# Two attention layers on one core: values of a chunk in one beat, layer-1 products in the other

## The chip, the core and the metric

The kernel runs on one core of a Trainium2 chip. The metric is the device time in microseconds (us) of one execution. A core has five engines with a queue each: TensorE (PE in the profile, with its weight loads as PEld), VectorE (DVE), ScalarE (ACT), GpSimd (POOL) and SyncE (SP), which here issues nearly all DMAs. Every engine works through its own queue in order and waits, by semaphores, for the others. Matmul results land in PSUM, from which VectorE and ScalarE read; everything else is in SBUF.

## The reference

The input x is 8 batches x 2048 nodes x 256 features in fp32, with one 2048 x 2048 adjacency matrix for all batches. Two layers follow, each x = layernorm(x + layer(x, adj)).

```
# layer 0: 4 heads of 64; softmax inside each chunk of 256 keys, summed over the 8 chunks
scores = clip(einsum('bhnd,bhjcd->bhnjc', q, kc) / 8, -10, 10)
scores = where(mask == 0, -10, scores)
ctx    = einsum('bhnjc,bhjcd->bhnd', softmax(scores, axis=-1), vc)
out    = layernorm(ctx @ Wo.T + bo + x) * gamma + beta
# layer 1: graph attention, one softmax over all 2048 neighbours
Wh = h @ W
e  = leaky_relu(s_i[:, :, None] + s_j[:, None, :], 0.2), -inf where not adjacent
out = elu(softmax(e) @ Wh)
```

## The kernel before

**Layer 0.** Work is cut into J = batch x block of 512 queries x chunk of 256 keys: 8 x 4 x 8 = 256 pairs of beats. A beat handles half a chunk, 128 keys, for all 4 heads and 512 queries; the first half of a chunk is the even beat (`half == 0`), the second the odd one. In each beat:

- TensorE computes transposed scores `sc` (L682): keys on partitions, two heads side by side in the array (64 rows each), two PSUM tiles `sc` of 128 x 1024 (2 buffers in all, so the next beat's first tile waits for this beat's first exponential and the second for the second);
- VectorE clips and masks each tile with one instruction against the mask `mk`, the "cap" (L692);
- ScalarE takes the exponential of each into `e` (L695).

What the exponentials of a chunk are multiplied with comes one pair later (`prev`): three column-tiled products (4 heads x 32 columns, L708), each 16 matmul passes into one PSUM tile `m` of 128 x 512. Part 2 multiplies by ones and gives the denominators; parts 0 and 1 are the two 32-wide halves of the values. Before, parts 2 and 0 run in the even beat, part 1 in the odd. The pool `ps_m` of `m` has two buffers, shared by everything else that needs a PSUM tile for a moment: projections (`pq`, `pk`, `pv`, `po`, `pw`), transposes (`pt`, `psj`, `pab`), row sums (`pr`). ScalarE copies part 2 to `ds` (L722) and parts 0 and 1 to `un` (L716). The denominators then go through a DMA into a dense layout `dc` (L724), VectorE's reciprocal at the end of the even beat (L730), DMAs to HBM `rd` and back, spread over partitions, `r` (L732, L736); two beats later VectorE scales `un` by `r` (L743), and POOL adds it to the context `ctxT` (L744).

**Layer 1** runs one batch behind, in steps (class `Step`), one for 128 keys x 512 queries; 16 steps make a block, 4 blocks a batch. `begin_beat` hands out 1.5 steps a beat (1.1 in the last batch), that is one and two in turn. A step goes through four stages, in successive beats: `low` (ScalarE, L517) in the beat it is taken; `leaky` and `edges` (VectorE, L521 and L526) in the next, before and behind the caps; `weights` (ScalarE exponential, L530, and the POOL sum `acc`, L539) at the start of the third; `product` (TensorE, L549; L564 in the last batch) at the end of that third beat, in `end_beat`. The step's tile `w` comes from a pool of 5 buffers. Products of a block add up in one PSUM tile `us` (pool `ps_u`, one buffer). With a block's last product ScalarE copies `us` to `hx` (L575), and generators in the list `fins` finish the block in later beats. Generators in `ahead` (`prelude`) prepare a batch's layer 1; between a batch's last block and the next batch's first step, layer 1 is idle for some 18 to 20 of 64 beats.

**What sets the order.** There is no scheduler (`manual_schedule`): each engine's queue has the instructions in the order in which Python emits them. Within a beat that is: `begin_beat` (weights, lows, leakies), scores, caps, exponentials, `middle_of_beat` (edges), value products with their copies, `end_beat` (products, one step of each generator, then what is due in `agenda`). So ScalarE's queue in an even beat holds weights, lows, exponential, exponential, copy `ds`, copy `un`.

Of the kernel before, what the change touches and what calls it, by code (L numbers as in the profile page):

```python
# [9 lines left out]
F32 = mybir.dt.float32  # L10
# [3 lines left out]
AF = mybir.ActivationFunctionType  # L14
# [5 lines left out]
P = 128  # L20
# [8 lines left out]
def tile_adj_attention__then__gat(  # L29
# [35 lines left out]
    nc = tc.nc  # L65
    B, N, F = x.shape
    H, D = 4, 64
# [3 lines left out]
    IB = 512  # L71
    NIB = N // IB
    TPB = IB // P
    NPAIR = H // 2
# [12 lines left out]
    one = ctx.enter_context(tc.tile_pool(name="one", bufs=1))  # L87
    two = ctx.enter_context(tc.tile_pool(name="two", bufs=2))
    three = ctx.enter_context(tc.tile_pool(name="three", bufs=3))
    five = ctx.enter_context(tc.tile_pool(name="five", bufs=5))  # L90
    eight = ctx.enter_context(tc.tile_pool(name="eight", bufs=8))
    ctx.enter_context(tc.manual_schedule())

# [413 lines left out]
    class Step:  # L507
# [5 lines left out]

        def low(self):
            k, c = self.k, self.c
            self.w = five.tile([P, IB], F32, tag="w", name=f"w{self.name}")
            nc.scalar.activation(self.w, k["ab"][:, 1, :], AF.Identity, bias=k["sj"][:, 1, c : c + 1])  # L517

        def leaky(self):
# [77 lines left out]
    def at(when, fn):  # L597
        agenda.setdefault(when, []).append(fn)

    def begin_beat(rate):  # L600
        nonlocal l1_live, credit, lows, edged, weighted, leaking
        weighted, edged = edged, []
        for s in weighted:
            s.weights()
        leaking, lows = lows, []
        credit = min(credit + rate, 2.0)
        while l1_live and credit >= 1.0:
            s = next(l1, False)
            if s is False:
                l1_live = False  # L610
            elif s is None:
                break
            else:
                credit -= 1.0
                lows.append(s)
                s.low()
        for s in leaking:
            s.leaky()
# [4 lines left out]
            s.edges()  # L623
        edged = leaking

    def end_beat():

        nonlocal weighted
        for s in weighted:
            s.product()  # L630
        weighted = []
        for gens in (ahead, fins):
            for g in list(gens):
                if next(g, g) is g:
                    gens.remove(g)
        for fn in agenda.pop(beat, []):
            fn()

    leaking = []


    first_m0 = two.tile([P, HT, IB], I8, tag="mask0", name="mk0_0_0_0")
# [7 lines left out]
    fins.append(far_made())  # L650

    prev = None
    v = None
    total = B * NIB * NCH
    mk0 = {}
    for J in range(total + 1):
# [5 lines left out]
        for half in range(2):  # L662
            c = 2 * j + half
            if live:

                if c % HT == 0:
                    if b == 0:
                        mk = blocks0[ib, c // HT]
                    else:
                        mk = mk0.pop((b, ib, c // HT))  # L670
                if c % HT == 1:
                    n = (b * NIB + ib) * 2 + c // HT + 1
                    nb, nib, nhf = n // (2 * NIB), n // 2 % NIB, n % 2
                    if 0 < nb < B:
                        mk0[nb, nib, nhf] = mask_block(0, nib, nhf, f"{nb}_{nib}_{nhf}")
            begin_beat(RATE if b < B - 1 else LAST_RATE)
            if live:
                scs = []
                for hp in range(NPAIR):
                    sc = ps_s.tile([P, 2, IB], F32, tag="sc", name=f"sc{b}_{ib}_{c}_{hp}")  # L680
                    for h in range(2):
                        nc.tensor.matmul(  # L682
                            sc[:, h, :],
                            kT[h * D : (h + 1) * D, hp, ts(c, P)],
                            qT[h * D : (h + 1) * D, hp, :],
                            start=True,
                            stop=True,
                        )
                    scs.append(sc)
                cap = mk[:, c % HT, :].unsqueeze(1).to_broadcast([P, 2, IB])  # L690
                for hp in range(NPAIR):
                    nc.vector.scalar_tensor_tensor(scs[hp], scs[hp], -CLIP, cap, ALU.max, ALU.min)  # L692
                for hp in range(NPAIR):
                    e = eight.tile([P, 2, IB], F32, tag="e", name=f"e{b}_{ib}_{c}_{hp}")
                    nc.scalar.activation(e, scs[hp], AF.Exp)  # L695
                    cur["es"].append(e)
            middle_of_beat()

            if prev is not None:
                if half == 0:  # L700
                    prev["un"] = two.tile([P, 2, IB], F32, tag="un", name=f"un{prev['name']}")
                for part in ((2, 0), (1,))[half]:
                    m = ps_m.tile([P, IB], F32, tag="m", name=f"u{prev['name']}_{part}")
                    for i in range(2):
                        pc = 2 * prev["j"] + i
                        for h in range(H):
                            f0 = h * D + part * DH
                            nc.tensor.matmul(  # L708
                                m[h * DH : (h + 1) * DH, :],
                                prev["v"][:, pc, f0 : f0 + DH] if part < 2 else ones[:, 0:DH],  # L710
                                prev["es"][2 * i + h // 2][:, h % 2, :],
                                start=(i == 0),
                                stop=(i == 1),
                            )
                    if part < 2:
                        nc.scalar.copy(prev["un"][:, part, :], m)  # L716
                    else:

                        ds = two.tile([P, IB], F32, tag="ds", name=f"ds{prev['name']}")
                        nc.scalar.copy(ds, m)  # L722
                        dc = two.tile([P, IB // DH], F32, tag="dc", name=f"dc{prev['name']}")
                        nc.sync.dma_start(  # L724
                            out=dc, in_=ds.rearrange("(h m) (n w) -> h m n w", m=DH, n=DH)[:, 0, :, :]
                        )
                        prev["dc"] = dc

                        def inverse(p=prev):
                            nc.vector.reciprocal(p["dc"], p["dc"])  # L730
                            p["rd"] = dram3.tile([H, IB], F32, tag="rd", name=f"rd{p['name']}")
                            nc.sync.dma_start(out=p["rd"].rearrange("h (m w) -> (h m) w", m=DH), in_=p["dc"])  # L732

                        def spread(p=prev):
                            p["r"] = two.tile([P, IB], F32, tag="r", name=f"r{p['name']}")
                            nc.sync.dma_start(out=p["r"], in_=p["rd"].unsqueeze(1).to_broadcast([H, DH, IB]))  # L736

                        def scaled(p=prev):
                            r2 = p["r"].unsqueeze(1).to_broadcast([P, 2, IB])
                            if p["j"] == 0:  # L740
                                nc.vector.tensor_mul(p["ctxT"], p["un"], r2)
                            else:
                                nc.vector.tensor_mul(p["un"], p["un"], r2)  # L743
                                nc.gpsimd.tensor_add(p["ctxT"], p["ctxT"], p["un"])  # L744
                            if p["j"] == NCH - 3:
                                fins.append(fin(p["b"], p["ib"], p["ctxT"]))

                        at(beat, inverse)
                        at(beat, spread)
                        at(beat + 2, scaled)  # L750

            end_beat()
            if half == 1:


                if live and j == NCH - 2 and J + 2 < total:
                    nb, nib = (b, ib + 1) if ib + 1 < NIB else (b + 1, 0)
                    xq = xT_tile(nb, nib, "q")
                if live and j == NCH - 1 and J + 1 < total:
                    if nb != b:  # L760
                        tiles = [xT_tile(nb, i, "k") for i in range(2)]
                    qT = make_qT(nb, nib, xq)
# [12 lines left out]
    while agenda or fins or ahead or l1_live or l1_open():  # L775
        begin_beat(1.0)
        middle_of_beat()
        end_beat()
        beat += 1


# [42 lines left out]
```

## Time and profile before

| | us |
|---|---|
| median of 3 runs | 4520.47 (4513.71 to 4526.38) |
| the profiled execution | 4511.16 |
| its span, first to last instruction | 4509.4 |
| TensorE busy | 4099.9 (91%) |
| VectorE busy | 3395.1 (75%) |
| ScalarE busy | 2596.6 (58%) |
| POOL busy | 1780.3 (39%) |
| granted TensorE clock, mean share of full speed | 0.971 |

A busy share is an average over stages that differ: layer 0 alone at first, both layers in most beats, layer 1 alone in the last 310 us. Lines of a timeline give the start in us, the duration in us, the engine, the line of the kernel, the operation, the tiles written and read, their shape, and how many such instructions the line merges; in brackets the idle time before, and what ended it. One fp32 matmul of the program is two passes in the profile, so the 8 rows of `sc` in a beat are 4 matmuls, the 16 rows of one part of the values 8, and the 8 rows of one layer-1 product step 4. The times below are those of the profiled execution.

### The profile page before, as it was taken

The page shows a single profiled execution, that of the slowest core. Times are in us where ns is not written, and L with a number is a line of the kernel's source. Part 1 is how long each engine was busy: PE and PEld are TensorE (multiplying, and loading weights), DVE is VectorE, ACT ScalarE, POOL GpSimd, SP SyncE. Part 2 cuts the span into 40 slices and gives each one's busy share as a digit, 9 for nine tenths or more (in the row PEclk, how much of TensorE's full clock was granted, in tenths as well). Part 3 has the DMA queues.
Part 4 walks back from the last instruction along what each step waited for, and adds up shares of the span by engine and source line. Part 5 has one row for each costly group of instructions (what it writes and reads, how often), then busy time and mean ns, then how long its engine had stood idle before and what let it go on. Part 6 is the DMA issues. An engine that isn't in the chain of part 4 may idle for free. (4 is left out here: it accounts for less than half of the span.)

```text
span 4509.4 us, 61241 instructions
## 1 busy us (share of the span) xinstructions
PE 4099.9 (91%) x23052; PEld 1922.9 (43%) x23052; DVE 3395.1 (75%) x4497; ACT 2596.6 (58%) x3847; POOL 1780.3 (39%) x906
## 2 busy tenths in 40 slices
PE   7888889999999999999999999999989999899767
PEld 3222334444344443445434453444434444344546
DVE  4666469985699658995599856998569975798686
ACT  4565446665556655665556655566555665566445
POOL 0222224553255423553344542455325543355511
PEclk9999999999999999999999999999999999999988
DMA  5444233322322223223233223332333232332241
GB/s 173 151 157 132 92 100 101 99 83 81 102 86 89 90 73 112 89 78 88 91 94 100 79 73 103 97 104 64 94 100 87 91 95 74 105 95 77 66 132 55
DMA packets 264233, 433.98 MB, mean 96 GB/s; under 512 B 85504, under 2 KB 120576, under 8 KB 260864
## 3 DMA queue, kind: packets, MB, share of 16 engines
q1 hardware_dynamic: 263936, 430.06, 30.6%
q8 instruction: 181, 2.97, 0.3%
q14 instruction: 116, 0.95, 0.1%
HBM read 358.48 MB, written 69.40 MB: 95 GB/s over the span
## 5 line engine op out<-in xcount | busy, mean ns | idle before, releaser
L695 ACT ACTIVATE e<-sc 128x1024 f32<-128x1024 f32 x1024 | 1035.7, 1020 | 1125.2 <-DVE sc L692 1080.7
L692 DVE SCALAR_TENSOR_TENSOR sc<-sc,mk 128x1024 f32<-128x1024 f32 x1024 | 1205.4, 1221 | 581.4 <-PE sc L682 314.4
L682 PE MATMUL sc<-qT,kT 64*128 64x512 f32 x4096 | 1064.5, 633 | 111.3 <-ACT e L695 108.9
L744 POOL TENSOR_TENSOR ctxT<-ctxT,un 128x1024 f32<-128x1024 f32 x224 | 563.5, 2516 | 1215.4 <-DVE un L743 1109.7
L708 PE MATMUL u<-e,v 128*32 128x512 f32 x8192 | 982.4, 597 | 0.0
L549 PE MATMUL us<-wh,w 128*128 128x256 f32 x3584 | 874.2, 393 | 75.5 <-ACT w L530 57.9
L549 PEld LDWEIGHTS us<-wh,w 128*128 128x128 f32 x3584 | 662.3, 192 | 417.8 <-ACT w L530 115.3
L539 POOL TENSOR_TENSOR acc<-acc,w 128x512 f32<-128x512 f32 x392 | 607.0, 1548 | 567.1 <-ACT w L530 557.2
L682 PEld LDWEIGHTS sc<-qT,kT 64*128 64x128 f32 x4096 | 346.8, 189 | 634.7 <-ACT e L695 320.1
L521 DVE SCALAR_TENSOR_TENSOR w<-ab,sj,w 128x512 f32<-128x512 f32 x512 | 578.3, 1150 | 29.8 <-ACT w L517 29.7
L708 PEld LDWEIGHTS u<-e,v 128*32 128x32 f32 x8192 | 240.2, 110 | 662.0 <-issue 549.3
L526 DVE TENSOR_TENSOR w<-w,mk 128x512 f32<-128x512 f32 x512 | 474.2, 946 | 41.6 <-DMA mk<-mask 38.9
L708 PE MATMUL u<-e,ones 128*32 128x512 f32 x4096 | 498.0, 604 | 0.0
L425 DVE CUSTOM_DVE_ANT_0 fb<-sj_row,fb 128x1024 bf16<-128x1024 f32 x256 | 402.7, 1581 | 5.7 <-DMA fb<-far 5.5
L530 ACT ACTIVATE w<-w 128x512 f32<-128x512 f32 x512 | 310.7, 631 | 90.1 <-DVE w L526 89.6
L517 ACT ACTIVATE w<-ab,sj 128x512 f32<-128x512 f32 x512 | 353.3, 716 | 13.4 <-PE us L564 6.2
L716 ACT COPY un<-u 128x512 f32<-128x512 f32 x512 | 300.9, 588 | 52.2 <-PE u L708 49.9
L743 DVE TENSOR_TENSOR un<-un,r 128x1024 f32<-128x1024 f32 x224 | 276.8, 1236 | 62.3 <-DMA r<-rd 59.6
L708 PEld LDWEIGHTS u<-e,ones 128*32 128x32 f32 x4096 | 107.9, 110 | 357.4 <-issue 315.7
L730 DVE RECIPROCAL dc<-dc 128x16 f32<-128x16 f32 x256 | 64.0, 250 | 186.3 <-DMA dc<-ds 168.1
L564 PE MATMUL us<-wh,w 128*128 128x257 f32 x512 | 128.5, 412 | 46.0 <-ACT w L530 45.7
L480 POOL TENSOR_TENSOR hx<-hx,hr 128x1024 f32<-128x1024 f32 x32 | 91.6, 2862 | 191.7 <-DVE hx L479 191.7
(97 smaller groups left out, 3153.6 us busy)
## 6 DMA issues: line engine op xcount, KB each, us to landing
r<-rd SPq DMA_DIRECT2D x256, 256.0 KB
fb<-far SPq DMA_DIRECT2D x256, 256.0 KB
mk<-mask SPq DMA_DIRECT2D x120, 512.0 KB
xT_k<-in_xT_dram SPq DMA_DIRECT2D x32, 512.0 KB
xT_q<-in_xT_dram SPq DMA_DIRECT2D x32, 512.0 KB
rawf<-in_adj_dram SPq DMA_DIRECT2D x16, 1024.0 KB
xT_v<-in_xT_dram SPq DMA_DIRECT2D x32, 512.0 KB
x<-in_x_dram SPq DMA_DIRECT2D x32, 512.0 KB
```

The lines of the kernel that those rows point to most:

```text
L425: nc.vector.tensor_tensor_reduce(out=fbs[2 * TPB * ib + n], in0=sj_row[:, ts(n % 2, HN)], in1=fbs[2 * TPB * ib + n], scale=1.0, scalar=2 * ...
L517: nc.scalar.activation(self.w, k["ab"][:, 1, :], AF.Identity, bias=k["sj"][:, 1, c : c + 1])
L521: nc.vector.scalar_tensor_tensor(self.w, k["ab"][:, 0, :], k["sj"][:, 0, c : c + 1], self.w, ALU.add, ALU.max)
L526: nc.vector.tensor_tensor(self.w, self.w, self.k["mks"][self.c // HT][:, self.c % HT, :], ALU.min)
L530: nc.scalar.activation(self.w, self.w, AF.Exp)
L539: nc.gpsimd.tensor_add(k["acc"], k["acc"], self.w)
L549: nc.tensor.matmul(k["us"][:, t, :], self.w[:, ts(t, P)], k["wh"][:, c, 0:F], start=(first and t % 2 == 0), stop=last, skip_group_check=True,)
L682: nc.tensor.matmul(sc[:, h, :], kT[h * D : (h + 1) * D, hp, ts(c, P)], qT[h * D : (h + 1) * D, hp, :], start=True, stop=True,)
L692: nc.vector.scalar_tensor_tensor(scs[hp], scs[hp], -CLIP, cap, ALU.max, ALU.min)
L695: nc.scalar.activation(e, scs[hp], AF.Exp)
L708: nc.tensor.matmul(m[h * DH : (h + 1) * DH, :], prev["v"][:, pc, f0 : f0 + DH] if part < 2 else ones[:, 0:DH], prev["es"][2 * i + h // 2][ ...
L744: nc.gpsimd.tensor_add(p["ctxT"], p["ctxT"], p["un"])
```

## The change

Four things change together.

1. `values` (the old loop body as a function) runs parts 2, 0 and 1 all in the even beat if layer 1 has steps in hand (`leaking or weighted`). Otherwise part 1 stays in the odd beat.
2. `end_beat` issues products only in odd beats (`products`); steps weighted in the even beat wait in `weighted` for it, so an odd beat holds three steps, an even one none. After the last layer-0 beat every beat issues them.
3. The copies off PSUM are interleaved with the exponentials: exponential, part, exponential, part, part; in an odd beat without layer 1, exponential, part 1, exponential. `middle_of_beat` moves ahead of them, which changes nothing on any one engine's queue by itself.
4. The pool of `w` has 6 buffers in place of 5.

```diff
-    five = ctx.enter_context(tc.tile_pool(name="five", bufs=5))
+    six = ctx.enter_context(tc.tile_pool(name="six", bufs=6))
...
     def begin_beat(rate):
-        weighted, edged = edged, []
-        for s in weighted:
+        for s in edged:
             s.weights()
+        weighted, edged = weighted + edged, []
...
-    def end_beat():
+    def end_beat(products):
         nonlocal weighted
-        for s in weighted:
-            s.product()
-        weighted = []
+        if products:
+            for s in weighted:
+                s.product()
+            weighted = []
...
+    def values(p, part):
+        if part == 2:
+            p["un"] = two.tile([P, 2, IB], F32, tag="un", name=f"un{p['name']}")
+        m = ps_m.tile([P, IB], F32, tag="m", name=f"u{p['name']}_{part}")
...
-                for hp in range(NPAIR):
-                    e = eight.tile([P, 2, IB], F32, tag="e", name=f"e{b}_{ib}_{c}_{hp}")
-                    nc.scalar.activation(e, scs[hp], AF.Exp)
+            middle_of_beat()
+            if prev is not None and half == 0:
+                parts = [2, 0, 1]
+                later = [] if leaking or weighted else [parts.pop()]
+            else:
+                parts, later = later, []
+            for n in range(3):
+                if live and n < NPAIR:
+                    e = eight.tile([P, 2, IB], F32, tag="e", name=f"e{b}_{ib}_{c}_{n}")
+                    nc.scalar.activation(e, scs[n], AF.Exp)
                     cur["es"].append(e)
-            middle_of_beat()
-            if prev is not None:
-                if half == 0:
-                    prev["un"] = two.tile([P, 2, IB], F32, tag="un", name=f"un{prev['name']}")
-                for part in ((2, 0), (1,))[half]:
...
-            end_beat()
+                if n < len(parts):
+                    values(prev, parts[n])
+            end_beat(half == 1)
```

What `values` does for a part, its matmuls, its copy and the denominators' way through DMA and reciprocal, is the old code unchanged (the matmuls are L651 of the new kernel, the copies L665 for `ds` and L659 for `un`).

More of the change, by code (lines that the diff above doesn't have):

```diff
@@ L515, in low @@
             k, c = self.k, self.c
-            self.w = five.tile([P, IB], F32, tag="w", name=f"w{self.name}")
+            self.w = six.tile([P, IB], F32, tag="w", name=f"w{self.name}")
             nc.scalar.activation(self.w, k["ab"][:, 1, :], AF.Identity, bias=k["sj"][:, 1, c : c + 1])
@@ L639, in tile_adj_attention__then__gat, with inverse, spread, scaled @@
     leaking = []
+    def values(p, part):
+        if part == 2:
+            p["un"] = two.tile([P, 2, IB], F32, tag="un", name=f"un{p['name']}")
+        m = ps_m.tile([P, IB], F32, tag="m", name=f"u{p['name']}_{part}")
+        for i in range(2):
+            pc = 2 * p["j"] + i
+            for h in range(H):
+                f0 = h * D + part * DH
+                nc.tensor.matmul(
+                    m[h * DH : (h + 1) * DH, :],
+                    p["v"][:, pc, f0 : f0 + DH] if part < 2 else ones[:, 0:DH],
+                    p["es"][2 * i + h // 2][:, h % 2, :],
+                    start=(i == 0),
+                    stop=(i == 1),
+                )
+        if part < 2:
+            nc.scalar.copy(p["un"][:, part, :], m)
+        else:
+            ds = two.tile([P, IB], F32, tag="ds", name=f"ds{p['name']}")
+            nc.scalar.copy(ds, m)
+            dc = two.tile([P, IB // DH], F32, tag="dc", name=f"dc{p['name']}")
+            nc.sync.dma_start(
+                out=dc, in_=ds.rearrange("(h m) (n w) -> h m n w", m=DH, n=DH)[:, 0, :, :]
+            )
+            p["dc"] = dc
+            def inverse():
+                nc.vector.reciprocal(p["dc"], p["dc"])
+                p["rd"] = dram3.tile([H, IB], F32, tag="rd", name=f"rd{p['name']}")
+                nc.sync.dma_start(out=p["rd"].rearrange("h (m w) -> (h m) w", m=DH), in_=p["dc"])
+            def spread():
+                p["r"] = two.tile([P, IB], F32, tag="r", name=f"r{p['name']}")
+                nc.sync.dma_start(out=p["r"], in_=p["rd"].unsqueeze(1).to_broadcast([H, DH, IB]))
+            def scaled():
+                r2 = p["r"].unsqueeze(1).to_broadcast([P, 2, IB])
+                if p["j"] == 0:
+                    nc.vector.tensor_mul(p["ctxT"], p["un"], r2)
+                else:
+                    nc.vector.tensor_mul(p["un"], p["un"], r2)
+                    nc.gpsimd.tensor_add(p["ctxT"], p["ctxT"], p["un"])
+                if p["j"] == NCH - 3:
+                    fins.append(fin(p["b"], p["ib"], p["ctxT"]))
+            at(beat, inverse)
+            at(beat, spread)
+            at(beat + 2, scaled)
     first_m0 = two.tile([P, HT, IB], I8, tag="mask0", name="mk0_0_0_0")
@@ L652, in tile_adj_attention__then__gat @@
     prev = None
+    later = []
     v = None
@@ L692, in tile_adj_attention__then__gat @@
                     nc.vector.scalar_tensor_tensor(scs[hp], scs[hp], -CLIP, cap, ALU.max, ALU.min)
-                for hp in range(NPAIR):
-                    e = eight.tile([P, 2, IB], F32, tag="e", name=f"e{b}_{ib}_{c}_{hp}")
-                    nc.scalar.activation(e, scs[hp], AF.Exp)
-                    cur["es"].append(e)
-            middle_of_beat()
-            if prev is not None:
-                if half == 0:
-                    prev["un"] = two.tile([P, 2, IB], F32, tag="un", name=f"un{prev['name']}")
-                for part in ((2, 0), (1,))[half]:
[L703 to L750, printed above, removed]
@@ L752, in tile_adj_attention__then__gat @@
-            end_beat()
+            middle_of_beat()
+            if prev is not None and half == 0:
+                parts = [2, 0, 1]
+                later = [] if leaking or weighted else [parts.pop()]
+            else:
+                parts, later = later, []
[3 more added lines that the diff above has]
+                    nc.scalar.activation(e, scs[n], AF.Exp)
+                    cur["es"].append(e)
+                if n < len(parts):
+                    values(prev, parts[n])
@@ L777, in tile_adj_attention__then__gat @@
         middle_of_beat()
-        end_beat()
+        end_beat(True)
         beat += 1
```

## The prediction

> **What bounds the kernel now.** I read the page's busy shares, then stretches, then the timeline of single beats, then the waits. One stretch in which layer 1 runs (columns: stretch, its length, busy us of PE, PEld, DVE, ACT, POOL, granted clock, DMA):
>
> ```profile
> PE 4099.9 (91%) x23052; PEld 1922.9 (43%) x23052; DVE 3395.1 (75%) x4497; ACT 2596.6 (58%) x3847; POOL 1780.3 (39%) x906
> 1778.00:2071.00 293.00, 281.61 (x1635) 138.50 (x1635) 273.30 (x346) 186.07 (x281) 161.22 (x84) 0.99 0.28 84
> ```
>
> TensorE is 96% busy there and VectorE 93%. TensorE is the bound, VectorE is close behind, and one can run ahead of the other only by what the buffers between them allow. TensorE's rows with no wait show what a change of matmul shape costs:
>
> ```profile
> 4129.52 1.99 PE L682 MATMUL sc<-qT,kT 64*128 64x512 f32 x8
> 4131.44 1.92 PE L708 MATMUL u<-e,ones 128*32 128x512 f32 x16
> 4133.18 1.90 PE L708 MATMUL u<-e,v 128*32 128x512 f32 x16
> 4135.01 2.00 PE L549 MATMUL us<-wh,w 128*128 128x256 f32 x8
> 4136.94 1.99 PE L682 MATMUL sc<-qT,kT 64*128 64x512 f32 x8
> ```
>
> From start to start: scores 1.92, denominators 1.74, values 1.83, one product step 1.93. Inside a group four 512-column passes start 0.43 apart, so 1.72 is the pure pace of each; a second product step in a row adds 1.72 too. What is over is paid at the seams: 0.20 for each visit to scores, 0.14 (0.02 + 0.11, rounded) to values, 0.21 to products.
>
> An even beat in which VectorE is late, from TensorE, VectorE and ScalarE in order of time:
>
> ```profile
> 2422.44 1.99 PE L682 MATMUL sc<-qT,kT 64*128 64x512 f32 x8
> 2427.65 2.35 DVE L692 SCALAR_TENSOR_TENSOR sc<-sc,mk 128x1024 f32<-128x1024 f32 x2
> 2427.93 1.99 PE L549 MATMUL us<-wh,w 128*128 128x256 f32 x8
> 2428.90 2.15 ACT L695 ACTIVATE e<-sc 128x1024 f32<-128x1024 f32 x2 [2.53 <-DVE sc L692]
> 2430.95 0.58 ACT L722 COPY ds<-u 128x512 f32<-128x512 f32 x1
> 2431.68 1.06 PE L351 MATMUL pt<-ident,y 128*128 128x128 f32 x8 [1.76 <-ACT ds L722]
> ```
>
> The caps start 5.2 us after the scores (1.25 when VectorE waits for TensorE). TensorE does the product step meanwhile; the transposes, third user of the two PSUM buffers in this beat, wait 1.76 us for the denominators' copy. An odd beat without layer 1:
>
> ```profile
> 2181.24 1.99 PE L682 MATMUL sc<-qT,kT 64*128 64x512 f32 x8
> 2183.16 1.92 PE L708 MATMUL u<-e,v 128*32 128x512 f32 x16
> 2183.75 2.15 ACT L695 ACTIVATE e<-sc 128x1024 f32<-128x1024 f32 x2 [1.82 <-DVE sc L692]
> 2185.80 0.58 ACT L716 COPY un<-u 128x512 f32<-128x512 f32 x1
> 2185.96 0.19 PEld L682 LDWEIGHTS sc<-qT,kT 64*128 64x128 f32 x2 [0.65 <-ACT e L695]
> ```
>
> The second half of the next scores starts 0.06 us after the second exponential ends: nothing may come between the exponentials there for free. And from the list of waits (total us, times, longest):
>
> ```profile
> DVE dc L730 <- DMA dc<-ds: 168.1, 108, 4.7
> PE pt L351 <- ACT ds L722: 22.4, 22, 2.3
> PE us L549 <- ACT hx L575: 17.6, 6, 2.9
> ```
>
> **The change, part by part.**
>
> 1. *Fewer seams: a gain.* Counted in TensorE's program order, the visits to values fall from 512 to 359 and those to full-array work (products, projections, transposes) from 381 to 288; visits to scores stay. 153 x 0.14 + 93 x 0.20 = 40 us. Not in the trace is the seam from scores straight to products (152 times): from scores to values 0.12, from values to products 0.22; leaving scores costs 0.10 and entering products 0.10, so I take 0.20. The ends give a gain of 37 to 52.
>
> [...]
>
> 2. *Third value product waits for the denominators' copy: a loss.* With layer 1 running, an even beat is scores, denominators, values 0, values 1 on two PSUM buffers. Values 1 are due 1.92 + 2 x 1.73 = 5.4 us after the scores start; the buffer is free when the denominators are copied, behind the first exponential, behind the first cap. With caps starting c after the scores: exponential ends c + 2.28, copy c + 2.75 (0.58, less 0.11 by which ScalarE's instructions overlap), TensorE goes on 0.15 later: c + 2.9. The wait is c - 2.5. Before, the product step covered this; it is now in the odd beat. Queued behind: values 1, the next scores, so the next caps. Of the 145 even beats with layer 1, 95 have c over 2.5, and the waits sum to 148 us if each is paid alone.
>
> They are not: after TensorE has waited, VectorE is that much less late. In the stretch from 1778 to 2163 us, c by runs (a run starts where VectorE waits for TensorE): 5.1 4.9 | 1.25 3.7 4.4 | 1.25 5.2 3.6 2.6 2.7 | 1.25 5.0 4.5 4.2 3.6 | 1.25 1.5 3.9 | 1.25 | 1.25 3.7. Alone they sum to 22.1; the largest of each run gives 2.6 + 1.9 + 2.7 + 2.5 + 1.4 + 1.2 = 12.3 (56%). Some runs already hold a wait that hangs on the same late exponentials and goes with it: 2.9 for the hx copy in the second, 1.76 for the transposes in the third, 1.5 for the output projection in the fourth. That leaves 2.6 + 0 + 0.9 + 1.0 + 1.4 + 1.2 = 7.1 (32%). Of 148 this is 47 to 83 us; I take 60. Ends: nothing, if VectorE comes to be less late (rival A), and 148.
>
> [...]
>
> 3. *Copies between exponentials where layer 1 is idle: a loss.* There the second value product stays in the odd beat; ScalarE does exponential, copy, exponential. The copy moves the second exponential by 0.47, or by about 0.75 where it also waits for the product (in the row above it can start at 2185.15, so the exponential ends near 2186.7 and not 2185.9). Odd beats without layer 1 or other TensorE work: 14 of 66 as tight as the row, 14 x 0.75 = 10; 34 with caps 0.2 to 1.2 later, where the earlier denominators win part back, 34 x 0.3 = 10; 18 later ones, and 21 even beats whose next scores already end on the second exponential: 39 x 0.47 = 18. Seven projections that wait for the odd copy get it 1.0 earlier: -7. Sum 31, between -10 (earlier denominators pay it all) and 50.
>
> 4. *Block ends in the middle of a group of three: a loss.* The one PSUM tile of products is copied (hx, 1.01 us) behind both exponentials before the next block's first product. Program order has such a boundary inside a group 6 times before, each a wait of 2.9; after, the same 6, and 6 new ones after a group's first step. There, as at 2040.8 us, the product is done 3.75 after the scores, the second exponential 5.2, hx 6.2 plus 0.15: 2.6 each, 16 us; ends 0 and 6 x 4.
>
> 5. *Costed at nothing.* The sixth w buffer: a low of an even beat reuses the buffer of the first step of the odd group before, multiplied 3.75 us after that beat's scores, while ScalarE gets to the low after the second exponential, 4.7 at the earliest. If that cover goes, 0.7 us a beat. SP, VectorE and POOL keep their order but for one block in each batch that now ends a beat later: the load of its residual, its reciprocal, min/max and residual sum and its store move by a beat, past two leaky, two cap and two edge steps on VectorE and one acc sum on POOL, 1.2 us each at most, with a block's 10 beats to spare; the denominators' DMA keeps its place on SP and is only released earlier.
>
> Sum: -40 + 60 + 31 + 16 = +67 us. The profiled execution took 4511.16 us (span 4509.4); that gives 4578. It stands 9.3 below the median of the runs, 4520.47, so 4588.
>
> **Rivals.**
>
> A, faster: the denominators' copy and DMA leave one exponential (1.02 us) earlier. VectorE waited 168 us for them in 108 beats, in order, ahead of the next caps. If c falls by 2 us in even beats, the 148 of part 2 shrink to 14 (from the same 145 beats), a third to a half of it paid: 6; part 3 goes to -5, part 4 to 13. -40 + 6 - 5 + 13 = -26, so 4494. It decides at a fall of about 1.5. For it: 168 us. Against: in the late beats VectorE hardly waits (93% busy), and only 3.7 of the 168 lie in 1778 to 2071.
>
> B, worse: each wait is paid alone, because other work makes VectorE late anew in each pair: -37 + 148 + 45 + 20 = +176, so 4696. Against: the runs above are series of falling c.
>
> C, VectorE becomes the bound where layer 1 runs: neither the seams nor the waits of part 2 count, 31 + 16 = +47, so 4567. For it: 93%. It lies inside my own range.
>
> D, a draw: half of A's fall (1 us: 64 alone, 27 paid): -40 + 27 + 5 + 13 = +5, so 4525.
>
> **How the numbers follow.** My forecast with C 0.61, A 0.21, D 0.08, B 0.10. Runs of this kernel differ by about 0.3% (4514 to 4526), the least that can be told from no change. Faster 0.21, same 0.08, slower 0.71. The range, 4478 to 4665, reaches over A's likely end and two thirds of the way to B; the forecast's own is 4545 to 4640.
>
> **What would show it.** Right: a wait of values 1 (L651) for the ds copy of 60 to 110 us in all; score groups behind products at 5.4 + 1.92 for three steps; score waits on exponentials above the present 109 us; hx waits of 12 times. Wrong: caps in even beats mostly under 2.5 us after the scores; a busy PE that falls by far more than 40 us, or not at all; VectorE's wait for denominators gone and the pair of beats at 14.5 us where it is now 14.8 at best.

## The result, and the profile after

| | before | after |
|---|---|---|
| median, us | 4515.1 (4513.2 to 4526.4, 6 runs) | 4545.0 (4535.0 to 4552.2, 6 runs) |
| profiled execution, us | 4511.16 | 4548.67 |
| its span, us | 4509.4 | 4546.8 |

The changed kernel takes 1.006 of the time before, 95% interval 1.0043 to 1.0076: 30 us slower by the medians, 37.4 by the spans of the profiled executions. Slower was the likely sign; the forecast of +67 was nearly twice what the profile shows. From here on the sums go against the 37.4.

The page after, first TensorE's share and then the costliest groups (busy us, mean ns of one, idle us before them and what ended most of it; L651 are the values, L737 the scores, L549 the layer-1 products, L248 the projections):

```profile
PE 4072.6 (90%) x23052; PEld 1935.7 (43%) x23052; DVE 3394.6 (75%) x4497; ACT 2596.0 (57%) x3847; POOL 1818.6 (40%) x906
...
L737 PE MATMUL sc<-qT,kT 64*128 64x512 f32 x4096 | 1060.4, 629 | 120.6 <-ACT e L759 118.3
...
L651 PE MATMUL u<-e,v 128*32 128x512 f32 x8192 | 969.6, 597 | 101.2 <-ACT ds L665 101.0
L549 PE MATMUL us<-wh,w 128*128 128x256 f32 x3584 | 838.7, 388 | 78.3 <-ACT w L530 52.2
```

TensorE is busy 27 us less than the 4099.9 before, with the same 23052 matmuls, and the program is longer: what was saved in work came back as waiting. From the list of waits after (total us, times, longest):

```profile
PE sc L737 <- ACT e L759: 118.3, 149, 5.7
DVE dc L673 <- DMA dc<-ds: 106.2, 66, 5.6
PE u L651 <- ACT ds L665: 101.0, 77, 2.4
PE pk L248 <- DMA xT_k<-in_xT_dram: 53.0, 10, 6.3
PE us L549 <- ACT hx L575: 26.0, 13, 2.2
```

Four of these stood in the list of before with other numbers: scores for exponentials 108.9, `dc` for its DMA 168.1, `pk` for its load 38.4, products for `hx` 17.6. The wait of the values is new.

This is what it looks like, in an even beat with VectorE late (start, duration, engine, line; lines of other work left out):

```profile
1889.57 1.92 PE L651 MATMUL u<-e,ones 128*32 128x512 f32 x16
...
1891.31 1.90 PE L651 MATMUL u<-e,v 128*32 128x512 f32 x16
...
1892.82 2.35 DVE L747 SCALAR_TENSOR_TENSOR sc<-sc,mk 128x1024 f32<-128x1024 f32 x2
1894.07 1.02 ACT L759 ACTIVATE e<-sc 128x1024 f32<-128x1024 f32 x1 [2.52 <-DVE sc L747]
1894.99 0.58 ACT L665 COPY ds<-u 128x512 f32<-128x512 f32 x1
...
1895.62 1.92 PE L651 MATMUL u<-e,v 128*32 128x512 f32 x16 [2.41 <-ACT ds L665]
```

The denominators are multiplied by 1891.3, and their copy needs 0.58 us, yet it starts at 1894.99: ScalarE takes its queue in order, and in front of the copy stands an exponential that waits for the late cap. The values therefore start 4.31 us after the group before them in place of 1.73. That is 2.58 more, while the bracket shows 2.41: each such wait of this trace costs about 0.17 us beyond its line.

Where nothing is late, the saving on seams is what was counted. A pair of beats in which layer 1 runs, TensorE alone:

```profile
1928.79 1.99 PE L737 MATMUL sc<-qT,kT 64*128 64x512 f32 x8
1930.71 5.45 PE L549 MATMUL us<-wh,w 128*128 128x256 f32 x24
1936.09 1.99 PE L737 MATMUL sc<-qT,kT 64*128 64x512 f32 x8
1938.00 1.92 PE L651 MATMUL u<-e,ones 128*32 128x512 f32 x16
1939.74 3.62 PE L651 MATMUL u<-e,v 128*32 128x512 f32 x32
1943.29 1.99 PE L737 MATMUL sc<-qT,kT 64*128 64x512 f32 x8
```

The odd beat takes 7.30 and the even one 7.20, together 14.50; the tightest pair of before took 7.41 + 7.42 = 14.83.

To place the 37.4 us, the table sums the lengths of beats (from the start of one group of scores to the next) in the trace, apart for pairs of beats in which products of layer 1 run and for the others:

| profiled execution, difference to before, us | pairs with layer 1 | pairs without | tail |
|---|---|---|---|
| the changed kernel | +65.0 | -28.1 | +0.5 |

So the part forecast as a loss where layer 1 is idle was a gain. And one loss was priced at nothing. It sits in the last beat of each batch, where the next batch's `qT` and `kT` are projected. These seven beats sum to 213.5 us before and to 231.9 after. At the fourth batch change, first SyncE's queue after, then TensorE:

```profile
2083.49 0.54 SPq L679 DMA_DIRECT2D r<-rd  x1
2088.98 0.38 SPq L485 DMA_DIRECT2D out_dram<-hx  x1
2089.41 0.50 SPq L315 DMA_DIRECT2D x<-in_x_dram  x1
2089.97 2.15 SPq L120 DMA_DIRECT2D xT_k<-in_xT_dram  x3
```

```profile
2096.45 7.99 PE L248 MATMUL pk<-xT_k,WT_k 128*128 128x512 f32 x11 [6.10 <-DMA xT_k<-in_xT_dram]
```

The store of a layer-1 block, L485, waits nearly 5 us on SyncE for the block's normalisation, and the loads of `xT_k` wait behind it although they need nothing from it. TensorE stands 6.10 us. The beat starts at 2079.55, so the loads leave 10.4 us into it. The same place before:

```profile
2074.18 0.38 SPq L485 DMA_DIRECT2D out_dram<-hx  x1
2074.66 0.46 SPq L732 DMA_DIRECT2D rd<-dc  x1
2077.30 0.54 SPq L736 DMA_DIRECT2D r<-rd  x1
2077.90 0.47 SPq L315 DMA_DIRECT2D x<-in_x_dram  x1
2078.42 4.17 SPq L120 DMA_DIRECT2D xT_k<-in_xT_dram  x3
```

```profile
2086.49 7.72 PE L248 MATMUL pk<-xT_k,WT_k 128*128 128x512 f32 x11 [4.30 <-DMA xT_k<-in_xT_dram]
```

There the beat started at 2071.27. The block had ended a beat earlier, its store left 2.9 us into this beat, ahead of the load of `r`, and the loads of `xT_k` left 7.2 us into it. Six of the seven batch changes are like this one, with the loads 10.4 us into the beat after; at the first, layer 1 has no block to store yet.

### The profile page after: what moved, and what is told of

It reads as the page before. It is cut to its first block, busy times and chain, and to the rows that moved or that the text cites. A ratio compares the mean times of both kernels' runs of the same rounds, so it can differ in the third digit from the quotient of the medians.

```text
span 4546.8 us, 61195 instructions
## 1 busy us (share of the span) xinstructions
PE 4072.6 (90%) x23052; PEld 1935.7 (43%) x23052; DVE 3394.6 (75%) x4497; ACT 2596.0 (57%) x3847; POOL 1818.6 (40%) x906
## 4 chain that ended last, share of the span: by engine, by line
PE 52%; DVE 21%; DMA 10%; ACT 8%; issue 6%; POOL 1%; SPq 0%; DVEq 0%; ACTq 0%; POOLq 0%
PE u L651 14%; PE sc L737 12%; PE us L549 11%; DVE sc L747 7%; DVE w L521 3%; PE pw L384 3%; DVE fb L425 3%; PE pk L248 3%; PE pv L266 2%; PE po L327 2%; ACT e L759 2%; DMA rd<-dc 2%; DVE w L526 2%; PE pq L248 2%; DMA mk<-mask 2%
## 5 line engine op out<-in xcount | busy, mean ns | idle before, releaser
L737 PE MATMUL sc<-qT,kT 64*128 64x512 f32 x4096 | 1060.4, 629 | 120.6 <-ACT e L759 118.3
L687 POOL TENSOR_TENSOR ctxT<-ctxT,un 128x1024 f32<-128x1024 f32 x224 | 577.4, 2578 | 1274.7 <-DVE un L686 1003.7
L651 PE MATMUL u<-e,v 128*32 128x512 f32 x8192 | 969.6, 597 | 101.2 <-ACT ds L665 101.0
L549 PE MATMUL us<-wh,w 128*128 128x256 f32 x3584 | 838.7, 388 | 78.3 <-ACT w L530 52.2
L539 POOL TENSOR_TENSOR acc<-acc,w 128x512 f32<-128x512 f32 x392 | 627.4, 1601 | 538.6 <-ACT w L530 527.4
L549 PEld LDWEIGHTS us<-wh,w 128*128 128x128 f32 x3584 | 669.6, 191 | 301.5 <-issue 110.8
L737 PEld LDWEIGHTS sc<-qT,kT 64*128 64x128 f32 x4096 | 344.7, 187 | 688.9 <-ACT e L759 330.8
L521 DVE SCALAR_TENSOR_TENSOR w<-ab,sj,w 128x512 f32<-128x512 f32 x512 | 557.3, 1109 | 29.0 <-ACT w L517 29.0
L651 PEld LDWEIGHTS u<-e,v 128*32 128x32 f32 x8192 | 247.5, 110 | 762.0 <-issue 532.5
L651 PE MATMUL u<-e,ones 128*32 128x512 f32 x4096 | 500.1, 606 | 0.0
L526 DVE TENSOR_TENSOR w<-w,mk 128x512 f32<-128x512 f32 x512 | 462.0, 922 | 45.0 <-DMA mk<-mask 42.2
L425 DVE CUSTOM_DVE_ANT_0 fb<-sj_row,fb 128x1024 bf16<-128x1024 f32 x256 | 416.1, 1633 | 6.6 <-DMA fb<-far 6.2
L659 ACT COPY un<-u 128x512 f32<-128x512 f32 x512 | 301.4, 589 | 178.4 <-PE u L651 178.2
L651 PEld LDWEIGHTS u<-e,ones 128*32 128x32 f32 x4096 | 108.0, 110 | 358.8 <-issue 316.8
L665 ACT COPY ds<-u 128x512 f32<-128x512 f32 x256 | 148.9, 581 | 59.7 <-PE u L651 53.7
L248 PE MATMUL pk<-xT_k,WT_k 128*128 128x512 f32 x256 | 135.4, 694 | 53.0 <-DMA xT_k<-in_xT_dram 53.0
```

The source lines that it names most:

```text
L248: nc.tensor.matmul(pm, WT[name][:, k, ts(o, P)], xt[:, k, :], start=(k == 0), stop=(k == KC - 1))
L425: nc.vector.tensor_tensor_reduce(out=fbs[2 * TPB * ib + n], in0=sj_row[:, ts(n % 2, HN)], in1=fbs[2 * TPB * ib + n], scale=1.0, scalar=2 * ...
L521: nc.vector.scalar_tensor_tensor(self.w, k["ab"][:, 0, :], k["sj"][:, 0, c : c + 1], self.w, ALU.add, ALU.max)
L526: nc.vector.tensor_tensor(self.w, self.w, self.k["mks"][self.c // HT][:, self.c % HT, :], ALU.min)
L539: nc.gpsimd.tensor_add(k["acc"], k["acc"], self.w)
L549: nc.tensor.matmul(k["us"][:, t, :], self.w[:, ts(t, P)], k["wh"][:, c, 0:F], start=(first and t % 2 == 0), stop=last, skip_group_check=True,)
```

## The experiments

Ten kernels were run, each timed together with the kernel before, to which its ratio refers. "Old places" below means: part 1 of the values in the odd beat, products in every beat, as before.

| kernel | edit | median, us | ratio to before (95%) |
|---|---|---|---|
| changed | | 4545.0 | 1.006 (1.0043 to 1.0076) |
| e1 | changed, copy `ds` ahead of the first exponential | 4485.3 | 0.9936 (0.992 to 0.9953) |
| e2 | changed, both exponentials ahead of all copies | 4674.1 | 1.0351 (1.0331 to 1.0371) |
| e3 | old places, copies interleaved | 4448.7 | 0.9847 (0.9822 to 0.9872) |
| e4 | changed, odd copy last | 4549.1 | 1.0081 (1.006 to 1.0102) |
| e5 | e1, early `xT_k` loads | 4416.6 | 0.9782 (0.9766 to 0.9798) |
| e6 | e3, products in odd beats | 4532.8 | 1.0036 (1.0023 to 1.005) |
| e7 | e3, all values in even beats | 4549.0 | 1.0075 (1.006 to 1.009) |
| e8 | e3, early `xT_k` loads | 4401.5 | 0.9748 (0.9733 to 0.9762) |
| e9 | changed, block stores a beat later | 4501.9 | 0.995 (0.9933 to 0.9967) |
| e10 | changed, early `xT_k` loads | 4474.2 | 0.9898 (0.9875 to 0.9921) |

### e1: the denominators' copy ahead of the exponentials

```diff
+            if prev is not None and half == 0 and (leaking or weighted):
+                values(prev, parts.pop(0))
+                parts = [None] + parts
...
-                if n < len(parts):
+                if n < len(parts) and parts[n] is not None:
```

> The changed kernel, but in even beats with layer 1 the denominators' copy stands ahead of both exponentials on ScalarE (copy, exponential, exponential, copy, copy). In the changed kernel's profile the beats with layer 1 took 65 us more than before, the others 28 less. Theory W: the 65 come from the third value product's wait for that copy (101 us), which stands behind an exponential and so behind VectorE's late caps. Then the copy ends 4.4 us after the scores start, ahead of the 5.4 at which it is wanted; the wait goes to under 10 us, and what is left where layer 1 runs is the seams' gain of 40 and some 10 for hx: 4455 to 4475 us. Rival C: VectorE is the bound there and the wait only fills time that TensorE would spend waiting for exponentials anyway; then the wait moves to the scores and the time stays at 4530 to 4545.

4485.3 us, 60 less than the changed kernel, and between the 4455 to 4475 of theory W and the 4530 to 4545 of rival C. Its list of waits:

```profile
ACT ds L665 <- PE u L651: 468.8, 167, 9.1
PE u L651 <- ACT ds L665: 13.7, 13, 1.4
```

The wait of the values is gone (101.0 to 13.7), so its cause was the copy's place in ScalarE's queue. ScalarE now waits for the copy's product itself, 468.8 us in all, and that costs little where the caps are late anyway. But the 87 us returned only 51 in the pairs with layer 1 (+65.0 to +13.6): transposes, output projections and `pab`, which no longer waited in the changed kernel, wait again (10.5, 8.6 and 4.5 us), and the seven last beats take 5 us more (237.1 against 231.9).

### e2: the copies behind both exponentials

```diff
-            for n in range(3):
-                if live and n < NPAIR:
+            for n in range(NPAIR):
+                if live:
...
-                if n < len(parts):
-                    values(prev, parts[n])
+            for part in parts:
+                values(prev, part)
```

> The changed kernel with both exponentials ahead of all copies, as before the change. Theory W: the denominators' copy comes one exponential (1.04 us) later, so the third product's wait, 101 us, grows to 150 to 200, and the 28 us gained where layer 1 is idle go: 4600 to 4650. Rival C: the wait is paid by nobody, and only the 28 go: 4570 to 4580. If the 28 have nothing to do with the interleaving, they stay.

4674.1 us, beyond the 4600 to 4650 expected. With the new places but the old order of copies, the values wait more often and longer:

```profile
PE u L651 <- ACT ds L665: 177.9, 89, 3.6
```

So the two halves of the change pull against each other: the interleaving is worth 129 us in the new places (4674 to 4545), and the places alone would have cost 3.5%. Not all of the 129 is waiting. TensorE's line of the page shows the same matmuls taking 55 us more than in the changed kernel (4072.6), at a granted clock of 0.959 in place of 0.973:

```profile
PE 4127.5 (88%) x23052; PEld 1957.1 (42%) x23052; DVE 3396.9 (73%) x4497; ACT 2610.3 (56%) x3847; POOL 1779.0 (38%) x906
```

### e3: the interleaving alone

```diff
-                later = [] if leaking or weighted else [parts.pop()]
+                later = [parts.pop()]
...
-            end_beat(half == 1)
+            end_beat(True)
```

and 5 buffers of `w`, as before.

> The interleaving alone: values and products in the places of before, copies between the exponentials in both beats, 5 w buffers. If the 28 us gained where layer 1 is idle are the interleaving's, and it costs nothing where layer 1 runs (the second exponential 0.6 later, with 2 us to spare), 4487 (4480 to 4495). If copies between exponentials delay the scores where layer 1 runs as well, 4515 or more.

4448.7 us: 1.5% faster than before, more than twice the gain expected. By pairs of beats it gains 36.1 us where layer 1 is idle and 22.7 where it runs. Its wait for denominators:

```profile
DVE dc L673 <- DMA dc<-ds: 104.8, 68, 4.3
```

Before it was 168.1: the copy `ds` leaves one exponential earlier, its DMA with it, and VectorE, whose reciprocal stands ahead of the next caps, waits 63 us less. Of these, 46 lie in pairs with layer 1 (55.6 to 9.4) and only 17 in the others (110.6 to 93.6). In the others something else falls as well: the waits of TensorE's projections, transposes and other small work for the copies `ds` and `un`, which free their PSUM buffers, go from 39.1 to 15.2 us.

### e4: the odd copy's place

```diff
-                parts, later = later, []
+                parts, later = [None] + later if later else [], []
```

with the same guard against `None` as in e1.

> The changed kernel, but in odd beats without layer 1 the copy of the value product stands behind both exponentials again (even beats unchanged). It asks which half of the interleaving gained the 28 us. If the earlier odd copy did, by freeing a PSUM buffer for projections behind it: 4545 plus 15 to 25, 4560 to 4570. If the earlier denominators in the even beat did, the odd copy was only in the way (0.3 to 0.75 in 48 beats), and it gets faster: 4525 to 4535.

4549.1 us, the changed kernel's time within its spread, so neither theory holds: whether the copy of part 1 stands between the exponentials of an odd beat or behind both makes no difference that can be seen in the time. In TensorE's waits of the pairs without layer 1 both theories show, and about cancel: with the copy last, scores wait 88.1 us for exponentials there (101.7 in the changed kernel), and small work waits 31.8 us for `ds` and `un` (12.9 in the changed kernel). The pairs without layer 1 stay 26.5 us shorter than before (28.1 in the changed kernel). In e2 the same pairs are 12.8 us longer than before, but TensorE stands as long there as before (184 against 185 us); the rest is the clock, 0.947 in place of 0.957. Together this puts the gain on the even beat, in which only `ds` has moved ahead, by one exponential.

### e6 and e7: each half of the new places alone

e6 is e3 with `end_beat(half == 1)` and 6 buffers; e7 is e3 with all values in the even beat where layer 1 runs.

> The interleaving alone (4449 us) plus products of layer 1 in odd beats only; values as before (two in the even beat, one in the odd), 6 w buffers. The seams alone: 93 fewer visits to full-array work at 0.20, -19. Against it the even beat has 5.4 us of matmuls and the odd one 9.2, so the next scores follow late exponentials in even beats (needed by 5.5, that is caps by 3.1 after the scores, mean 3.1): +45 as in my working for the third product, and the later block end +12 on SP. 4485 (4470 to 4500). If the beats' balance does not matter: 4430 to 4445.

> The interleaving alone (4449 us) plus all values in the even beat where layer 1 runs; products in every beat, 5 w buffers. Seams: 153 fewer visits to values at 0.14, -21. The third value product waits for the denominators' copy as in the changed kernel (101 us there, of which 51 to 60 came back when the copy was put first): +55; odd beats have 5.6 us of matmuls, so late exponentials there delay the next scores: +20. 4503 (4485 to 4520). If the wait is what costs and the odd beat is no matter: 4483.

4532.8 and 4549.0 us, both beyond what was expected (4470 to 4500 and 4485 to 4520): 84 and 100 above e3, where both together cost 96. The halves do not add up; the lists of waits show that each alone makes TensorE wait in its own way. One line of each list of waits, e6 first:

```profile
PE sc L737 <- ACT e L759: 153.0, 227, 5.8
```

```profile
PE u L651 <- ACT ds L665: 98.5, 82, 2.3
```

In e6 the odd beat holds values and three products, the even one neither products nor the second values. TensorE is through the even beat early, and there the next scores wait for its exponentials: 39.6 us of idle TensorE at the scores of odd beats where layer 1 runs, against 0.3 in e3. Where layer 1 runs, transposes and `pab` also wait 37.5 us in place of 7.7, and the seven last beats take 234.9 us in place of 212.8 (203.6 in e7). In e7 the values wait as in the changed kernel, and products, spread over all beats, wait for their weights as well (75.6 against 53.1).

### e5, e8, e10: the next batch's loads a beat earlier

```diff
+            if live and half == 0 and j == NCH - 1 and ib == NIB - 1 and b + 1 < B:
+                tiles = [xT_tile(b + 1, i, "k") for i in range(2)]
             end_beat(...)
...
-                    if nb != b:
-                        tiles = [xT_tile(nb, i, "k") for i in range(2)]
```

> The run with the denominators' copy first (4485 us), with the next batch's first two key loads issued a beat earlier on SP. Theory Q: with products only in odd beats the third block of each batch ends a beat later, and its result's store, which waits on SP for the normalisation, now stands ahead of those loads at the moment they are wanted (SP idle 4.9 us there, loads 3 us later, TensorE's wait for the key projection 44 us where layer 1 runs and 23 in the interleaving alone). Moved ahead of the store the loads are there in time: 4465 to 4473. Rival: the projection waits for PSUM or for the copies and the loads only show last: 4480 to 4490.

> The interleaving alone (4449 us) with the same loads a beat earlier. There no store stands in front of them; what is left of TensorE's waits for them is 40 us in all, of which the first batch's start cannot go: 4435 to 4445. If the loads bring nothing without the store, 4449.

> The changed kernel with the first two xT_k loads of the next batch issued a beat earlier, as in the two runs that had them before; the placements stay as changed. If the loads are worth the same wherever they are done, as on the version with the denominators' copy first (-69 us), 4476; if the 22 us by which that gain exceeded the one on the old placements (-47) hang on something else than SP, 4498. Either way the waits of pk for xT_k all but go and the wait of the values for the denominators' copy stays at about 100 us.

The two loads are worth 69 us on e1, 47 on e3 and 71 on the changed kernel, several times what was expected of the first two; on the changed kernel it is what the first theory of e10 named (4476, measured 4474.2). The seven last beats of a batch, summed: 212.8 in e3, 170.7 in e8; 231.9 in the changed kernel, 169.6 in e10. With the loads out early the two placements take the same time there. What the changed kernel had more than e3, 19 us in these beats, thus hangs on the loads and not on the work of the beat. In e8 little of the wait is left:

```profile
PE pk L248 <- DMA xT_k<-in_xT_dram: 11.6, 4, 6.2
```

e8, 4401.5 us, is the fastest version run, 2.5% under the kernel before: the old places, the copies interleaved, the two loads a beat earlier.

### e9: the store behind the loads

```diff
         normalize(hx, mv, rstd, f"c{b}_{ib}")
+        yield
         nc.sync.dma_start(out=out[b, ts(ib, IB), :].rearrange("(t p) f -> p t f", p=P), in_=hx)
```

> The changed kernel with the store of each finished layer-1 block (L485) issued one beat later, so that at the end of a batch it no longer stands ahead of the next batch's xT_k loads in SP's queue; nothing else moves. Theory S (the block that ends a beat later costs through this store): the loads go out some 3 us earlier in each of the 7 changes of batch, the waits of pk for xT_k fall from 53.0 to about 40 us, and with fewer half-pace passes behind them the kernel takes 4520 to 4530 us, that is 15 to 25 less than the changed kernel's 4545. Rival T (the loads are late anyway, the store only happens to stand there): 4542 to 4548. If the later store delays the next block's hx copy, a wait of hx for the store appears and the time goes above 4550.

4501.9 us, 43 less than the changed kernel by the medians, 34.6 by the spans of the profiled executions (that of e9 is the slowest of its seven). Theory S holds in kind, and its size was too small; the waits of `pk` for `xT_k` fall to 31.0 us, where 40 was expected. The seven last beats fall from 231.9 to 196.1, by 35.8, which is the whole gain. SyncE and TensorE at the same batch change:

```profile
2073.33 0.54 SPq L680 DMA_DIRECT2D r<-rd  x1
2073.92 0.47 SPq L315 DMA_DIRECT2D x<-in_x_dram  x1
2074.49 1.03 SPq L120 DMA_DIRECT2D xT_k<-in_xT_dram  x2
```

```profile
2082.34 7.96 PE L248 MATMUL pk<-xT_k,WT_k 128*128 128x512 f32 x18 [2.17 <-DMA xT_k<-in_xT_dram]
```

The beat starts at 2069.38: its loads leave 5.1 us into it, and TensorE waits 2.17 us where it had waited 6.10. That is 3.9 of the 7.0 us by which this beat gets shorter (33.83 to 26.87). The rest is the clock. Stretches of the projection in the changed kernel (length; busy us and instructions of PE, PEld, DVE, ACT, POOL; granted clock; share of DMA; GB/s), and below the first of e9:

```profile
2096.45:2098.45 2.00, 2.00 (x3) 0.97 (x4) 0.00 (x0) 0.00 (x0) 0.00 (x0) 0.50 0.86 332
2098.45:2100.45 2.00, 2.00 (x4) 0.85 (x3) 0.00 (x0) 0.21 (x1) 0.00 (x0) 0.50 0.00 1
2100.45:2102.45 2.00, 2.00 (x3) 0.67 (x2) 0.00 (x0) 0.48 (x1) 0.00 (x0) 0.50 0.00 0
2102.45:2104.45 2.00, 2.00 (x6) 0.93 (x5) 0.00 (x0) 0.69 (x1) 0.00 (x0) 0.97 0.17 20
```

```profile
2082.34:2084.34 2.00, 2.00 (x5) 1.03 (x6) 0.00 (x0) 0.00 (x1) 0.00 (x0) 1.00 0.54 206
2084.34:2086.34 2.00, 2.00 (x6) 0.82 (x5) 0.00 (x0) 0.97 (x2) 0.00 (x0) 1.00 0.00 0
```

After 6.10 us of standing, the clock granted to TensorE is 0.50 for some 6 us, which costs about 3 us of work at full clock; after 2.17 us it is 1.00 at once. In the kernel before, TensorE waited 4.30 us here, and the clock was 0.50 for some 5.5 us. Two reservations: e9 moves all 32 stores, so it also takes away waits on SyncE that the kernel before had (which is why its seven beats end 17 us under those of before), and the 18.4 us between before and after rest on the timeline and on the last-beat sums of e3, e8 and e10, not on e9 alone.

## Why the prediction was right or wrong

The sign held, the size did not: +67 was taken, and the profiled execution shows +37.4. Term by term:

| part | forecast | measured | from |
|---|---|---|---|
| 1 seams | -40 | -39 | 93 x 0.33 (14.83 - 14.50), and 60 x 0.14 |
| 2 values wait for `ds` | +60 | +85 | 101.0 + 77 x 0.17, less 29 of waits that went |
| 3 copies between exponentials | +31 | -28 | pairs without layer 1 |
| 4 block ends inside a group | +16 | +10 | 26.0 - 17.6, and 7 x 0.16 |
| 5 order on SyncE | 0 | +18 | seven last beats, 231.9 - 213.5 |
| not in the forecast | | -9 | products for their weights 57.9 to 52.2; `pq` with layer 1 3.4 to 0 |
| sum | +67 | +37 | profile: +37.4 |

The errors have both signs, +25, +18 and +1 against -59, -6 and -9. That the sum kept its sign and came within 30 us is in part luck: two of the five terms were wrong in kind.

**Part 1 held.** The seam from scores to products, not in the trace of before, is what was taken for it, 0.20 (0.10 out, 0.10 in), and the pair fell to the 14.5 named. In TensorE's program order after, the visits fell as counted, by 153 and 93; a pair that loses one of each saves 0.33. The 0.14 for the 60 that lose only a visit to values is the forecast's.

**Part 2 was right in mechanism and short in size.** The wait, its releaser and its total (60 to 110 us were named, 101.0 came) are as described. The step that failed is the reduction: only the largest of each run of late caps was to be paid, 32 to 56% of the full sum, and 77 waits were paid at 114 us against the 148 of each alone. What was taken off for waits that go with it did go: transposes, output projections and `pab` waited 30.3 us where layer 1 runs, and 1.6 after. That leaves 85, just above the 47 to 83. It was not the choice of the stretch: the pairs that were read, whose c - 2.5 summed to 22.1, sum to 17.2 after, where 12.3 was named. In its fourth run the caps start 4.97 and 4.44 us after the scores, as late as before (4.95, 4.46), and both waits are paid, 2.2 and 2.3 us; only from the third on are they earlier, 2.20 in place of 4.24. A wait of TensorE relieved VectorE less, and later, than was taken.

**Part 3 failed in sign, and this is the larger error.** The step was that a copy moves the second exponential by 0.47 to 0.75 us, 38 us in all, against which stood only 7 us for projections that get their buffer earlier; the earlier denominators came in as a smaller price in 34 beats and as the lower end, -10. In the pairs without layer 1 both sides show in TensorE's waits, in other sizes: scores wait 9 us more for exponentials (93.0 to 101.7), and small work waits 26 us less for `ds` and `un` (39.1 to 12.9). In all TensorE stands 20 us less there (185 to 165); the other 8 of the 28 are the same matmuls at a higher granted clock (0.957 to 0.967). By e4 and e2 the gain comes from the earlier copy `ds` in the even beat, and the odd copy's loss and gain cancel. What of it goes by the PSUM buffer that the copy frees, and what by its DMA and VectorE, stays open, as no run parts the two: VectorE's wait for `dc`, 168.1 us, had 110.6 of them in these pairs, and 95.7 after.

**Part 4** was named right (13 waits, 12 expected) and each was shorter, 2.0 us on average in the list in place of 2.6.

**Part 5 failed.** "With a block's 10 beats to spare" is true of the block and was the wrong question. What is queued behind its store on SyncE at a batch's end, the loads of `xT_k`, has nothing to spare: TensorE was already waiting 38.4 us for these loads before. e9 and e10, which move the store or the loads, take the 18 us away and more.

**The rivals.** A's mechanism, earlier denominators, is real but did not act as A has it: with layer 1 VectorE's wait for them all but goes (55.6 to 8.9 us), yet caps of even beats start 2.82 us after the scores on average in place of 3.10, far from the fall of 1.5 from which A decides. B is out, with 114 against 148 and no growth of the other terms. C, VectorE the bound with layer 1, is out: e1 removed the waits of TensorE and got 51 us back there. D needed half of A's fall, 1 us with layer 1; it was 0.28.

## What to carry to other kernels

When work of one engine is moved in a shared in-order queue, ask for each moved instruction what stands behind it and how much time that has, not how much time the moved work itself has; a store may wait with ease while the load behind it is already late. The place of the small copy `ds`, which frees a PSUM buffer and starts a DMA chain, was worth far more here than its 0.58 us: moved ahead of one exponential (the odd beat's copies with it) it was worth 65 us in the old places, and 129 where a third product waited for it. Where two edits come together, run each alone: the places cost 96 us and hid that the interleaving by itself gained 1.5%.

## What was not expected of the hardware

In some places a wait of TensorE cost more than its length. After 2.17 us of standing (e9, the batch change shown above) the granted clock was 1.00 at once; after 3.16 us (e3, same batch change) it was 0.54 and 0.60 in the next two stretches of 2 us, which are 3.4 us at half clock; after 4.30 us (before) 0.50 for about 5.5 us; after 6.10 us (after) 0.50 for about 6. The two stretches of e3:

```profile
2053.84:2055.84 2.00, 2.00 (x3) 0.97 (x4) 0.00 (x0) 0.00 (x0) 0.00 (x0) 0.54 0.33 126
2055.84:2057.84 2.00, 2.00 (x4) 0.73 (x4) 0.00 (x0) 0.38 (x1) 0.00 (x0) 0.60 0.00 0
```

The length of a wait alone does not tell what follows it. In the trace of before, TensorE waits 3.15 us for `xT_k` at the seventh batch change (3694.85 to 3698.00), as long as in e3 to 0.01 us, and the clock stays at 1.00. A wait of 2.10 us for `hTl` (3802.29 to 3804.38), shorter than the 2.17 of e9, is followed by 0.79, 0.50 and 0.85. The stretches of 2 us behind the one and the other:

```profile
3698.00:3700.00 2.00, 2.00 (x5) 1.03 (x6) 0.00 (x0) 0.01 (x1) 0.00 (x0) 1.00 0.34 130
3700.00:3702.00 2.00, 2.00 (x6) 0.82 (x5) 0.00 (x0) 0.97 (x2) 0.00 (x0) 1.00 0.00 0
```

```profile
3804.38:3806.38 2.00, 2.00 (x7) 1.69 (x8) 0.25 (x1) 0.38 (x1) 1.41 (x1) 0.79 0.65 242
3806.38:3808.38 2.00, 2.00 (x6) 1.61 (x5) 0.00 (x0) 0.37 (x1) 0.00 (x0) 0.50 0.01 2
3808.38:3810.38 2.00, 2.00 (x9) 1.22 (x10) 0.00 (x0) 0.93 (x3) 0.00 (x0) 0.85 0.00 0
```

What makes the difference was not shown.
